# Recommendation kernel: one gather of 128 per step of the item stage as 128 single-row transfers from SyncE and ScalarE

## The chip, the cores and the metric

The kernel runs on one core of one Trainium2 chip. The metric is the device time of one execution in microseconds (us); smaller is better. The engines are TensorE (PE), VectorE (DVE), ScalarE (ACT), GpSimd (POOL) and SyncE (SP). Transfers between DRAM and the on-chip memory are carried by 16 DMA engines. SP, ACT and POOL can each issue transfers.

## The reference

The inputs are 16384 users with a history of 100 items each and one target item, a table of 32 neighbours for each of 50001 items, and tables of embeddings. First every item gets two attention results over its neighbours:

```
def _neighbor_attn(E, near_full):
    V = E[near_full]                                     # 50001 x 32 x 32
    scores = einsum('nd,nkd->nk', E, V) / sqrt(32)
    w = softmax(scores, axis=-1)
    return einsum('nk,nkd->nd', w, V)
a_sus = _neighbor_attn(E_in, near_full)
a_inf = _neighbor_attn(E_out, near_full)
h = concat([E_hist[history], a_sus[history], a_inf[history]])   # 16384 x 100 x 128
t = concat([E_tgt[target], a_inf[target], a_sus[target]])       # 16384 x 128
z = relu(einsum('bld,hd->blh', h * t[:, None, :], W1) + b1)
exp_A = exp(einsum('blh,h->bl', z, W2[0])) * ((history != target) & (history != 0))
attn = exp_A / sum(exp_A, -1) ** 0.5
s = sum(h * attn[..., None])                             # one number
pred = sigmoid(cosine(s everywhere, t))                  # 16384
```

## The kernel before, in words

The program has two stages, one after the other: the **item stage**, which writes a row of 129 numbers per item into a table in DRAM, and the **user stage**, which gathers those rows for every user's history. Only the item stage is changed.

The two embedding tables E_in and E_out lie side by side in one table `egeo` in DRAM, 64 numbers (256 bytes) per item. The 50001 items are cut into 391 tiles of 128 items. Sixteen tiles make a group (`it`), for which `load` fetches the neighbour indices `nidx` in one transfer. Four tiles of a group make a **step** (`s`); there are 99 steps, the first 96 of four tiles, the last three of four, two and one (steps 96, 97, 98). A step's buffer `v` holds, for each of its 128 x 4 items, the 32 neighbours' rows of `egeo`; there are three such buffers in turn.

`gather(s)` fills `v` with indirect transfers from POOL. One of them (here: one gather) fetches one neighbour `k` for the 128 items of one tile `i`: 128 rows of 256 bytes. A step of four tiles takes 128 gathers. Then VectorE's `product(s)` multiplies `v` by the items' own rows (`own`, which ACT first copies into `small`, L162), and `attended(s)` does the rest on VectorE: sums (L181), maximum, subtraction, an exponential on ACT (L199), weights times `v` (L201), the sum over neighbours (L218), the division and the row's total (L227). `written(s)` has ACT copy half of the row (L232) and SP write the finished rows (`ttab` at L233, `table` at L236).

The order on every engine is the order of the calls, which the loop below writes out by hand. Each engine's instructions run in that order, and a semaphore holds an instruction until what it needs is done. The first gather of step `s` waits for the product of step `s - 1` (a dependency added by hand, "the gathers pause here"). The gathers of POOL share eight completion counters (DMASW0 to 7) in turn, and the transfers of SP and ACT together share eight others (DMAHW0 to 7). A transfer waits until the one before it on its counter has landed.

In one turn of the loop the calls are: the product of `s - 1`, the gathers of `s`, the index load of the next group (once in four steps), the own rows of `s + 2` (`own_of`), then the rest of the attention of `s - 1` and its writing.

In the user stage POOL gathers 128 rows of 516 bytes at a time from `table` (L358), 20 for each fifth of a block of 128 users, and one gather of target rows per block (L328); VectorE, SP (L403, L409, L455), TensorE (L418) and ACT work on them.

Of the kernel before, what the change touches and what calls it, by code (L numbers as in the profile page):

```python
# [10 lines left out]
F32 = mybir.dt.float32  # L11
I32 = mybir.dt.int32
U8 = mybir.dt.uint8
E = mybir.EngineType
AF = mybir.ActivationFunctionType
ALU = mybir.AluOpType
AX = mybir.AxisListType

P = 128
ITEMS = 50001  # L20
K = 32
G = 32
# [9 lines left out]
NSUB = 16  # L32
NT = -(-ITEMS // P)
ROWS = NT * P
STEP = 4

UC = B // P
BSUB = 4
# [19 lines left out]
def kernel(  # L58
# [13 lines left out]
    nc = tc.nc  # L72
# [4 lines left out]
    table = nc.dram_tensor("table_0", [ROWS, W], F32, kind="Internal").ap()  # L77
# [10 lines left out]
    def rows_of(t, it):  # L88
        n = min(NSUB, NT - it * NSUB)
        r = it * NSUB * P  # L90
        return t[r : r + n * P, :].rearrange("(p j) d -> p j d", j=n)

    steps = []
    for s in range(0, NT, NSUB):
        n, j = min(NSUB, NT - s), 0
        while j < n:
            left = NT - s - j
            m = min(STEP, n - j) if left > STEP else (left + 1) // 2
            steps.append((s // NSUB, j, m))
# [3 lines left out]
    with (  # L103
# [7 lines left out]
        its = {}  # L111
        subs = {}
# [4 lines left out]
        def load(it):  # L117
            n = min(NSUB, NT - it * NSUB)
            nidx = n_in.tile([P, NSUB, K], I32, name="nidx")
            nc.sync.dma_start(nidx[:, 0:n, :], rows_of(near, it))  # L120
            its[it] = nidx

        def copied(it):
            r0 = it * P * NSUB
            r1 = min(r0 + P * NSUB, ITEMS - 1)
            nc.sync.dma_start(ttab[r0:r1, 0:DE], etgt[r0:r1, :])
            if r1 == ITEMS - 1:
                nc.sync.dma_start(ttab[r1:ITEMS, 0:DE], etgt[r1:ITEMS, :])

        def own_of(s):  # L130
            it, j, m = steps[s]
            own = n_s.tile([P, STEP, 2 * G], F32, name="own", bufs=3)
            nc.sync.dma_start(own[:, 0:m, :], rows_of(egeo, it)[:, j : j + m, :])
            row = n_s.tile([P, STEP, W + G], F32, name="row", bufs=4)
            nc.sync.dma_start(row[:, 0:m, 1 : 1 + DE], rows_of(ehist, it)[:, j : j + m, :])
            subs[s] = {"own": own, "row": row}

        def gather(s):
            it, j, m = steps[s]
            v = n_v.tile([P, STEP, K, 2 * G], F32, name="v")  # L140
            subs[s]["v"] = v
            landed = subs[s]["landed"] = [
                nc.gpsimd.indirect_dma_start(  # L143
                    out=v[:, i, k, :],
                    out_offset=None,
                    in_=egeo,
                    in_offset=bass.IndirectOffsetOnAxis(ap=its[it][:, j + i, k : k + 1], axis=0),
                )
                for i in range(m)
                for k in range(K)  # L150
            ]
            if s > 0:
                tc.add_manual_dep(
                    landed[0].ins, subs[s - 1]["made"].ins.name, SYNC, reason="the gathers pause here"
                )

        def product(s):
            it, j, m = steps[s]
            u = subs[s]
            v, own = u["v"], u["own"]  # L160
            near_own = small[:, s % 2, 0 : m * 2 * G].rearrange("p (i d) -> p i d", i=m)
            nc.scalar.copy(near_own, own[:, 0:m, :])  # L162
            prod = n_p.tile([P, STEP, K, 2 * G], F32, name="pw")
            made = nc.vector.tensor_tensor(  # L164
                prod[:, 0:m],
                v[:, 0:m],
                near_own.rearrange("p i (o d) -> p i o d", o=1).to_broadcast([P, m, K, 2 * G]),
                ALU.mult,
            )
            for gone in u["landed"][:-1]:  # L170
                covered(made, gone)
            u["made"], u["prod"] = made, prod

        def attended(s):
            it, j, m = steps[s]
            u = subs[s]
            v, own, row, prod = u["v"], u["own"], u["row"], u["prod"]
            ex = small[:, s % 2, STEP * 2 * G : STEP * 2 * G + m * K * 2]
            low = small[:, s % 2, STEP * (2 * G + 2 * K) : STEP * (2 * G + 2 * K) + 2 * m]
# [49 lines left out]
        def written(s):  # L229
            it, j, m = steps[s]  # L230
            row = subs.pop(s)["row"]
            nc.scalar.copy(row[:, 0:m, W : W + G], row[:, 0:m, 1 + DE : 1 + DE + G])  # L232
            nc.sync.dma_start(  # L233
                rows_of(ttab, it)[:, j : j + m, DE:D], row[:, 0:m, 1 + DE + G : W + G]
            )
            nc.sync.dma_start(rows_of(table, it)[:, j : j + m, :], row[:, 0:m, 0:W])  # L236

        def covered(one, other):
            tc.declare_no_dep(one.ins, other.ins, reason="a later wait or one engine's order covers it")

        load(0)
        own_of(0)
        own_of(1)
        gather(0)
        copied(0)
        ps_c = held.enter_context(tc.tile_pool(name="ps_c", bufs=1, space=bass.MemoryType.PSUM))
        small = ps_c.tile([P, 2, 1024], F32, name="small")
        for s in range(len(steps) + 1):
            if s > 0:
                product(s - 1)  # L250
            if 0 < s < len(steps):
                gather(s)
            if s < len(steps):
                it, j, m = steps[s]
                if j == STEP and it + 1 < NITER:
                    load(it + 1)
                    copied(it + 1)
            if s + 2 < len(steps):
                own_of(s + 2)
            if s > 0:  # L260
                attended(s - 1)
                written(s - 1)

    pool = tc.tile_pool(name="uconst", bufs=1)
    const = ctx.enter_context(pool)
# [25 lines left out]
    def ring(name, n, *shape):  # L291
        return [u_h.tile([P, *shape], F32, name=f"{name}{i}") for i in range(n)]

    rows = ring("h", HB, LQ, W)
# [11 lines left out]
    with (  # L306
# [184 lines left out]
        for s in range(last + LAG + NCH):  # L491
            c, k = divmod(s, NCH)
            if s < last:
                if k == 0 and c % BSUB == 2 and 0 < c // BSUB and c // BSUB + 1 < UC // BSUB:
                    history_of(c // BSUB + 1)
                if k == 1 and c + 1 < USERS:
                    target_rows(c + 1)
                gather(s)
                blocks(s)
                move(s)  # L500
                if k == 3 and c + 1 < USERS:
                    target_work(c + 1)
            done, left = divmod(s - LAG - NCH, NCH)
            if 0 <= done < USERS and left == 0:
                weights(done)
            if s < last:
                hidden(s)
            if 0 <= s - LAG < last:
                partial(s - LAG)
                if (s - LAG) % NCH == NCH - 1:  # L510
                    folded((s - LAG) // NCH)
            if 0 <= done < USERS and left == 1:
                u = ended(done)
                waiting = (done, u)
            if 0 <= done < USERS and left == 2:
                summed(*waiting)
# [79 lines left out]
```

## Time and profile before

| What | Value |
|---|---|
| time, median of 3 runs | 35657.56 us (35654.25 to 35670.82) |
| the profiled execution's own time | 35666.41 us |
| its span, first to last instruction | 35664.6 us |
| item stage, to the last of its gathers | about 17500 us |
| user stage and the end | about 18160 us |
| gathers of the item stage (L143) | 12512 |
| gathers of the user stage (L358, L328) | 12928 |

The profile is of one execution. Its page gives the busy time of each engine, and the costliest groups of instructions by line: busy time, mean of one in ns, then the time for which the engine stood idle just before them and what ended most of it. Other views give the busy time of each engine in a stretch of the span, or the instructions in the order of time: start, duration, engine, line, operation, what is written and read, and in brackets the idle time before. SPq marks a transfer issued by SP: its time there is that of issuing it. Registers, waits and issuing are not counted as busy.

### The profile page before, as it was taken

To read this page: it belongs to the slowest core of one execution; us is meant where nothing else is said; L and a number is where in the kernel's file an instruction comes from. 1 tells how busy PE (TensorE), PEld (TensorE's weight loads), DVE (VectorE), ACT (ScalarE), POOL (GpSimd) and SP (SyncE) were. 2 spreads that over 40 slices of the span, in tenths; PEclk is the share of its full clock that TensorE was granted. 3 is DMA by queue.
4 is the path that set the end of the run, shared out by engine and by line. 5 is a ranking of instruction groups with operands and counts; after the bars stand their busy time and mean duration, and the time that the engine had idled before them with its cause. 6 is when DMAs were issued, how large, how long until landed. Compare 5 with 4: busy or idle time off the path is not lost.

```text
span 35664.6 us, 55636 instructions
## 1 busy us (share of the span) xinstructions
PE 5285.3 (15%) x6659; PEld 1829.6 (5%) x6659; DVE 11590.6 (32%) x5232; ACT 3500.3 (10%) x2864; POOL 25112.7 (70%) x25446
## 2 busy tenths in 40 slices
PE   0000000000000000000022222232222322222222
PEld 0000000000000000000001111111111111101011
DVE  2222222222222222222344444434444444444444
ACT  0000000000000000000011111111111111111112
POOL 7777777777777777777777666676666666667666
PEclk9999999999999999999865556666566655656556
DMA  1111111111111111111244444444444444444444
GB/s 31 28 28 28 29 28 28 28 29 28 28 28 29 28 28 28 29 28 27 66 140 139 141 140 142 142 136 141 140 142 141 141 140 141 142 138 144 139 140 138
DMA packets 1528347, 3043.73 MB, mean 85 GB/s; under 512 B 641056, under 2 KB 708256, under 8 KB 1446048
## 3 DMA queue, kind: packets, MB, share of 16 engines
q1 hardware_dynamic: 713888, 1774.76, 16.7%
q0 software_dynamic: 814080, 1265.42, 14.1%
q14 instruction: 325, 2.66, 0.0%
q8 instruction: 54, 0.88, 0.0%
HBM read 2154.17 MB, written 890.36 MB: 85 GB/s over the span
## 4 chain that ended last, share of the span: by engine, by line
issue 40%; POOL 22%; another core or an unknown queue 21%; DVE 10%; ACT 4%; PE 1%; DMA 1%; SPq 0%; ACTq 0%; POOLq 0%; DVEq 0%
POOL v L143 13%; POOL h L358 9%; ACT z L426 3%; DVE pw L164 2%; DVE att L218 2%; DVE pw L201 1%; DVE sc L181 1%; DVE x L374 1%; PE zb L418 1%; DVE xb L388 1%; DVE zT L435 1%; DVE part L436 1%; ACT z L429 0%; PE za L418 0%
## 5 line engine op out<-in xcount | busy, mean ns | idle before, releaser
L358 POOL DMA_INDIRECT h<-table,hidx x12800 | 12305.2, 961 | 5632.1 <-issue 4769.4
L143 POOL DMA_INDIRECT v<-in_egeo_dram,nidx x12512 | 12686.1, 1014 | 4810.1 <-issue 3767.3
L164 DVE TENSOR_TENSOR pw<-v,small 128x8192 f32<-128x8192 f32 (+1 forms) x99 | 849.5, 8580 | 13307.6 <-DMA v<-in_egeo_dram,nidx 13307.6
L418 PE MATMUL za<-xT,w1T 128*128 128x512 f32 x3840 | 3165.9, 991 | 10408.6 <-issue 3777.7
L435 DVE STREAM_TRANSPOSE zT<-z 128x2560 f32<-128x2560 f32 x640 | 1812.4, 2832 | 5759.5 <-ACT z L429 4637.2
L488 PE MATMUL tp<-ident,w_sb 128*128 128x128 f32 x1 | 0.4, 448 | 17510.0 <-DMA hidx<-in_history_dram 17510.0
L374 DVE TENSOR_TENSOR x<-h,tp 128x2560 f32<-128x2560 f32 x640 | 1801.3, 2814 | 2394.6 <-DMA h<-table,hidx 1960.4
L418 PE MATMUL zb<-xT,w1T 128*128 128x512 f32 x2560 | 2002.0, 926 | 2434.7 <-issue 1784.8
L426 ACT ACTIVATE z<-za,b_sb 128x1536 f32<-128x1536 f32 x640 | 986.3, 1541 | 8673.7 <-remote 5545.8
L388 DVE STREAM_TRANSPOSE xb<-x 128x2560 f32<-128x2560 f32 x640 | 1820.9, 2845 | 0.0
L436 DVE TENSOR_REDUCE part<-zT 128x80 f32<-128x2560 f32 x640 | 1804.8, 2820 | 21.9
L418 PEld LDWEIGHTS za<-xT,w1T 128*128 128x128 f32 x3840 | 1145.6, 318 | 12453.9 <-issue 9065.4
L429 ACT ACTIVATE z<-z,w_sb 128x2560 f32<-128x2560 f32 x640 | 1554.0, 2428 | 20.9
L199 ACT ACTIVATE small<-sc 128x256 f32<-128x256 f32 (+1 forms) x99 | 38.1, 385 | 15116.3 <-DVE sc L193 8230.1
L218 DVE TENSOR_REDUCE att<-pw 128x256 f32<-128x8192 f32 (+1 forms) x99 | 1347.2, 13608 | 0.0
L426 ACT ACTIVATE z<-zb,b_sb 128x1024 f32<-128x1024 f32 x640 | 713.0, 1114 | 5741.8 <-remote 4112.7
L488 PEld LDWEIGHTS tp<-ident,w_sb 128*128 128x128 f32 x1 | 0.2, 183 | 17509.9 <-issue 17509.9
L201 DVE TENSOR_TENSOR pw<-v,small 128x8192 f32<-128x8192 f32 (+1 forms) x99 | 849.3, 8579 | 51.1 <-issue 37.0
L418 PEld LDWEIGHTS zb<-xT,w1T 128*128 128x128 f32 x2560 | 662.6, 282 | 3673.0 <-issue 2864.4
L181 DVE TENSOR_REDUCE sc<-pw 128x256 f32<-128x8192 f32 (+1 forms) x99 | 849.3, 8578 | 3.4
L467 DVE TENSOR_TENSOR ea<-ea,keep 128x100 f32<-128x100 f32 x128 | 33.9, 265 | 2488.2 <-issue 2099.2
L232 ACT COPY row<-row 128x128 f32<-128x128 f32 (+1 forms) x99 | 29.6, 299 | 2295.9 <-issue 1737.4
(53 smaller groups left out, 1124.5 us busy)
## 6 DMA issues: line engine op xcount, KB each, us to landing
there<-xb SPq DMA_DIRECT2D x2560, 320.0 KB
xT<-there SPq DMA_DIRECT2D x640, 1280.0 KB
h<-table,hidx POOLq DMA_INDIRECT x12800
v<-in_egeo_dram,nidx POOLq DMA_INDIRECT x12512
table<-row SPq DMA_DIRECT2D x97, 258.0 KB
own<-in_egeo_dram SPq DMA_DIRECT2D x97, 128.0 KB
row<-in_ehist_dram SPq DMA_DIRECT2D x97, 128.0 KB
ttab<-row SPq DMA_DIRECT2D x97, 128.0 KB
```

The lines of the kernel that those rows point to most:

```text
L143: nc.gpsimd.indirect_dma_start(out=v[:, i, k, :], out_offset=None, in_=egeo, in_offset=bass.IndirectOffsetOnAxis(ap=its[it][:, j + i, k : ...
L164: made = nc.vector.tensor_tensor(prod[:, 0:m], v[:, 0:m], near_own.rearrange("p i (o d) -> p i o d", o=1).to_broadcast([P, m, K, 2 * G]), ...
L181: nc.vector.tensor_reduce(sc[:, 0:m].rearrange("p i k t -> p (i k t)"), prod[:, 0:m].rearrange("p i k (t d) -> p (i k t) d", t=2), AX.X, A ...
L218: nc.vector.tensor_reduce(att[:, 0:m], wv[:, 0:m].rearrange("p i k d -> p i d k"), AX.X, ALU.add)
L358: landed[s, q] = nc.gpsimd.indirect_dma_start(out=rows[s % HB][:, q, :], out_offset=None, in_=table, in_offset=bass.IndirectOffsetOnAxis(a ...
L374: made = nc.vector.tensor_tensor(x, h[:, :, 1:W], u["tp"].to_broadcast([P, LQ, D]), ALU.mult,)
L388: turn = nc.vector.transpose(xb.rearrange("p b q j -> p q b j"), x.rearrange("p q (b i) -> p q b i", b=Q))
L418: one = nc.tensor.matmul(z_ps[:, m - lo, :], w1T, xT[:, m * COLS : (m + 1) * COLS], start=True, stop=True,)
L426: nc.scalar.activation(z[:, lo * COLS : hi * COLS], z_ps.rearrange("h m n -> h (m n)"), AF.Relu, bias=b1_sb)
L429: nc.scalar.activation(z, z, AF.Copy, scale=w2_sb)
L435: nc.vector.transpose(zT.rearrange("p x i -> p (x i)"), zr[s % ZB])
L436: nc.vector.tensor_reduce(parts[c][:, :, k * LQ : (k + 1) * LQ], zT.rearrange("p (a q) i -> p a q i", a=Q), AX.X, ALU.add,)
```

## The change

In the steps 1 to 98, of the gathers of the first tile the last one (neighbour 31) is left out. In its place each of the 128 rows is fetched by a transfer of its own, of 256 bytes, from an address that is held in a register: the rows 0 to 63 by SP, 64 to 127 by ACT. The column of indices is loaded a second time per group, transposed (`ridx`, one tile per partition), and VectorE multiplies it by 256 into byte addresses (`addr`). SP and ACT load 16 addresses at a time from `addr` into registers and then issue 16 transfers. They do so for the step after the one whose gathers run. SP issues the first 32 of its rows ahead of the attention and writing of the step before, and the other 32 behind them; ACT issues all 64 behind them.

```
+RUN = 16
+ROWB = 2 * G * 4
+EARLY = {E.SP: P // 4, E.Activation: 0}
+FETCH = (E.SP, E.Activation,)
...
             nc.sync.dma_start(nidx[:, 0:n, :], rows_of(near, it))
+            ridx = n_in.tile([NSUB, P], I32, name="ridx")
+                nc.sync.dma_start(ridx[0:n, :], rows_of(near, it)[:, :, K - 1].rearrange("p j -> j p"))
+            addr = n_in.tile([NSUB, P], I32, name="addr")
+            nc.vector.tensor_scalar(addr[0:n, :], ridx[0:n, :], float(ROWB), None, ALU.mult)
...
+        def by_row(s):
+            return 1 if s > 0 else 0
+
+        def space(s):
+            subs[s]["v"] = n_v.tile([P, STEP, K, 2 * G], F32, name="v")
+
+        def fetch_rows(s, e, q0, q1):
+            it, j, m = steps[s]
+            if not by_row(s):
+                return
+            for q in range(e * P // 2 + q0, e * P // 2 + q1, RUN):
+                _, found = nc.values_load_multi_w_load_instructions(
+                    its[it]["addr"][j : j + 1, q : q + RUN],
+                    engines=[FETCH[e]],
...
+                for i, value in enumerate(found):
+                    engine_of[FETCH[e]].dma_start(
+                        subs[s]["v"][q + i : q + i + 1, 0, K - 1, :].bitcast(U8),
+                        flat[ds(value, ROWB)].rearrange("(o b) -> o b", o=1),
+                    )
...
                 for i in range(m)
-                for k in range(K)
+                for k in range(K - (i < by_row(s)))
...
             if s + 2 < len(steps):
                 own_of(s + 2)
+            if s + 1 < len(steps):
+                space(s + 1)
+                for e in range(len(FETCH)):
+                    fetch_rows(s + 1, e, 0, EARLY[FETCH[e]])
             if s > 0:
                 attended(s - 1)
                 written(s - 1)
+            if s + 1 < len(steps):
+                for e in range(len(FETCH)):
+                    fetch_rows(s + 1, e, EARLY[FETCH[e]], P // 2)
```

Three places of the built program show what moves. The lines of the changed program have other numbers: L161 loads addresses, L169 is a single-row transfer, L180 a gather. First ACT, between the row copy of one step and the exponential of the next. Before:

```order
L162 COPY small<-own 128x256
L199 ACTIVATE small<-sc 128x256
L232 COPY row<-row 128x4x32
L162 COPY small<-own 128x256
L199 ACTIVATE small<-sc 128x256
```

Now:

```order
L269 COPY row<-row 128x4x32
L161 TENSOR_LOAD addr
L169 DMA v<-in_egeo_dram 1x256 x16
L161 TENSOR_LOAD addr
L169 DMA v<-in_egeo_dram 1x256 x16
L161 TENSOR_LOAD addr
L169 DMA v<-in_egeo_dram 1x256 x16
L161 TENSOR_LOAD addr
L169 DMA v<-in_egeo_dram 1x256 x16
L199 COPY small<-own 128x256
L236 ACTIVATE small<-sc 128x256
```

Four loads and 64 transfers now stand between the row copy and the copy of the own rows that the next product reads. Second SP, in one turn of the loop, from the own rows of a later step on. Before:

```order
L133 DMA own<-in_egeo_dram 128x256
L135 DMA row<-in_ehist_dram 128x4x64
L233 DMA ttab<-row 128x4x64
L236 DMA table<-row 128x4x129
L133 DMA own<-in_egeo_dram 128x256
```

Now:

```order
L142 DMA own<-in_egeo_dram 128x256
L144 DMA row<-in_ehist_dram 128x4x64
L161 TENSOR_LOAD addr
L169 DMA v<-in_egeo_dram 1x256 x16
L161 TENSOR_LOAD addr
L169 DMA v<-in_egeo_dram 1x256 x16
L270 DMA ttab<-row 128x4x64
L273 DMA table<-row 128x4x129
L161 TENSOR_LOAD addr
L169 DMA v<-in_egeo_dram 1x256 x16
L161 TENSOR_LOAD addr
L169 DMA v<-in_egeo_dram 1x256 x16
```

Half of SP's rows stand ahead of the two writes and half behind them, and the next step's own rows behind those. Third POOL, where one step ends and the next begins (with the counters that each gather waits for; DVE is the product). Before:

```order
L143 DMA v_90<-in_egeo_dram,nidx_80 128x64 [waits DMASW7_49]
L143 DMA v_231<-in_egeo_dram,nidx_80 128x64 [waits DMASW0_49,DVE_49]
L143 DMA v_231<-in_egeo_dram,nidx_80 128x64 [waits DMASW1_49]
L143 DMA v_231<-in_egeo_dram,nidx_80 128x64 [waits DMASW2_49]
L143 DMA v_231<-in_egeo_dram,nidx_80 128x64 [waits DMASW3_49]
```

Now, from the fourth step on:

```order
L180 DMA v_1310<-in_egeo_dram,nidx_80 128x64 [waits DMASW4_49]
L180 DMA v_1854<-in_egeo_dram,nidx_755 128x64 [waits DMAHW3_49,DMAHW4_49,DMAHW2_49,DMAHW5_49,DMAHW1_49,DMAHW6_49,DMAHW0_49,DMAHW7_49,DMASW5_49,DVE_49]
L180 DMA v_1854<-in_egeo_dram,nidx_755 128x64 [waits DMASW6_49]
L180 DMA v_1854<-in_egeo_dram,nidx_755 128x64 [waits DMASW7_49]
L180 DMA v_1854<-in_egeo_dram,nidx_755 128x64 [waits DMASW0_49]
```

A step's first gather now waits for the eight counters of SP's and ACT's transfers too: the single rows of the step that last used this buffer. The product of a step waits for the same eight counters, for its own rows.

More of the change, by code (lines that the diff above doesn't have):

```diff
@@ L120, in load @@
             nc.sync.dma_start(nidx[:, 0:n, :], rows_of(near, it))
-            its[it] = nidx
+            ridx = n_in.tile([NSUB, P], I32, name="ridx")
+            with nc.allow_non_contiguous_dma(reason="one index of each item, for single rows"):
+                nc.sync.dma_start(ridx[0:n, :], rows_of(near, it)[:, :, K - 1].rearrange("p j -> j p"))
+            addr = n_in.tile([NSUB, P], I32, name="addr")
+            nc.vector.tensor_scalar(addr[0:n, :], ridx[0:n, :], float(ROWB), None, ALU.mult)
+            its[it] = {"nidx": nidx, "addr": addr}
         def copied(it):
@@ L136, in own_of @@
             subs[s] = {"own": own, "row": row}
+        flat = egeo.rearrange("r d -> (r d)").bitcast(U8)
+        engine_of = {E.SP: nc.sync, E.Activation: nc.scalar}
+        def by_row(s):
[10 more added lines that the diff above has]
+                    engines=[FETCH[e]],
+                    min_val=0,
+                    max_val=(ITEMS - 1) * ROWB,
+                    skip_runtime_bounds_check_because="every index is a row of the table",
+                )
[3 more added lines that the diff above has]
+                        flat[ds(value, ROWB)].rearrange("(o b) -> o b", o=1),
+                    )
         def gather(s):
             it, j, m = steps[s]
-            v = n_v.tile([P, STEP, K, 2 * G], F32, name="v")
-            subs[s]["v"] = v
+            if "v" not in subs[s]:
+                space(s)
+            v = subs[s]["v"]
             landed = subs[s]["landed"] = [
@@ L146, in gather @@
                     in_=egeo,
-                    in_offset=bass.IndirectOffsetOnAxis(ap=its[it][:, j + i, k : k + 1], axis=0),
+                    in_offset=bass.IndirectOffsetOnAxis(ap=its[it]["nidx"][:, j + i, k : k + 1], axis=0),
                 )
                 for i in range(m)
-                for k in range(K)
+                for k in range(K - (i < by_row(s)))
             ]
```

## The prediction

> **What bounds the kernel now.** I read the page's share by engine first, then the groups by line, then busy time by stage, then the order of time across one step of the item stage.
>
> ```profile
> PE 5285.3 (15%) x6659; PEld 1829.6 (5%) x6659; DVE 11590.6 (32%) x5232; ACT 3500.3 (10%) x2864; POOL 25112.7 (70%) x25446
> ...
> L358 POOL DMA_INDIRECT h<-table,hidx x12800 | 12305.2, 961 | 5632.1 <-issue 4769.4
> L143 POOL DMA_INDIRECT v<-in_egeo_dram,nidx x12512 | 12686.1, 1014 | 4810.1 <-issue 3767.3
> L164 DVE TENSOR_TENSOR pw<-v,small 128x8192 f32<-128x8192 f32 (+1 forms) x99 | 849.5, 8580 | 13307.6 <-DMA v<-in_egeo_dram,nidx 13307.6
> ```
>
> POOL is the busiest engine, nearly all of its work is gathers, and in the item stage VectorE's product (L164) waits 13307.6 us for their data. The stages by time:
>
> ```profile
> 0.00:17500.00 17500.00, 0.00 (x0) 0.00 (x0) 4121.43 (x981) 95.68 (x296) 12686.83 (x12518) 1.00 0.13 28
> 17500.00:35664.00 18164.00, 5285.32 (x6659) 1829.64 (x6659) 7469.19 (x4252) 3404.59 (x2568) 12425.88 (x12928) 0.61 0.48 140
> ```
>
> The columns are the stretch, its length, then busy time of PE, PEld, DVE, ACT and POOL, the clock, the DMA share and GB/s. In the item stage ACT works 95.68 us of 17500, VectorE 4121, and the DMA engines are 13% busy. So the item stage lasts as long as POOL takes over its gathers. How long one takes is seen in a single step, in the order of time:
>
> ```profile
> 1050.08 1.09 POOL L143 DMA_INDIRECT v<-in_egeo_dram,nidx  x1 [0.30 <-issue]
> 1052.62 8.69 DVE L164 TENSOR_TENSOR pw<-v,small 128x8192 f32<-128x8192 f32 x1 [136.12 <-DMA v<-in_egeo_dram,nidx]
> ...
> 1061.58 0.95 POOL L143 DMA_INDIRECT v<-in_egeo_dram,nidx  x1 [10.40 <-DVE pw L164]
> 1062.83 0.94 POOL L143 DMA_INDIRECT v<-in_egeo_dram,nidx  x1 [0.30 <-issue]
> ...
> 1143.96 1.01 POOL L143 DMA_INDIRECT v<-in_egeo_dram,nidx  x1 [0.30 <-issue]
> 1145.28 1.09 POOL L143 DMA_INDIRECT v<-in_egeo_dram,nidx  x1 [0.30 <-issue]
> 1146.68 1.10 POOL L143 DMA_INDIRECT v<-in_egeo_dram,nidx  x1 [0.30 <-issue]
> ...
> 1240.79 0.95 POOL L143 DMA_INDIRECT v<-in_egeo_dram,nidx  x1 [10.42 <-DVE pw L164]
> ```
>
> A step lasts 1240.79 - 1061.58 = 179.21 us: a pause of 10.4 us behind the product, then 66 gathers at (1143.96 - 1061.58) / 66 = 1.248 us each, then the rest at 1146.68 - 1145.28 = 1.40 us. And 179.21 / 128 = 1.400: the step is as long as 128 gathers at the slow pace with no pause at all. What the pause takes is given back by the quick ones behind it. The program's start says how much can be saved up so:
>
> ```profile
> 174.02 0.94 POOL L143 DMA_INDIRECT v<-in_egeo_dram,nidx  x1 [10.47 <-DVE pw L164]
> ...
> 326.30 0.94 POOL L143 DMA_INDIRECT v<-in_egeo_dram,nidx  x1 [0.30 <-issue]
> 327.55 1.06 POOL L143 DMA_INDIRECT v<-in_egeo_dram,nidx  x1 [0.30 <-issue]
> 328.91 1.09 POOL L143 DMA_INDIRECT v<-in_egeo_dram,nidx  x1 [0.31 <-issue]
> ```
>
> There the 128 gathers of step 0 and 123 of step 1 go quickly, to 327.55. The first began at 3.9, so 251 gathers took 323.6 us where 251 x 1.40 is 351.4: a reserve of 27.8 us, some 20 gathers. The rule that I take from these rows is a long-run price of 1.400 us per gather, with pauses up to the reserve free of charge. The user stage, with other rows and nearly four times the DMA share, has the same price: (12305.2 + 5632.1) / 12800 = 1.401. All 25440 gathers at 1.400 make 35616 of the span's 35664.6 us.
>
> **The change, part by part.** *Removed:* one gather in each of the steps 1 to 98, so 98 x 1.400 = **137.2 us**. The lower price would be the quick one, 98 x 1.248 = 122.3 us, if the count of slow ones did not fall; nothing if the long-run price were not paid per gather (second rival). I take 1.400, since both stages keep it whatever the pauses are.
>
> *Added on ACT:* 64 single-row transfers and 4 loads of 16 addresses per step, between its last item of a step (the row copy, L232) and the small copy for the next product (L162):
>
> ```profile
> 1094.91 0.30 ACT L232 COPY row<-row 128x128 f32<-128x128 f32 x1 [23.48 <-issue]
> 1094.91 0.69 DVE L227 TENSOR_REDUCE row<-row 128x4 f32<-128x512 f32 x1
> 1095.11 0.37 ACT L162 COPY small<-own 128x256 f32<-128x256 f32 x1
> 1095.23 0.37 SPq L233 DMA_DIRECT2D ttab<-row  x1
> 1095.28 0.94 POOL L143 DMA_INDIRECT v<-in_egeo_dram,nidx  x1 [0.30 <-issue]
> 1095.69 0.46 SPq L236 DMA_DIRECT2D table<-row  x1
> ```
>
> ACT is done at 1095.2, which is 33.9 us after the product's end (1052.62 + 8.69 = 1061.31). Then the small copy (0.4 us) is wanted only for the next product, whose 8.7 us end the cycle. With r for one row, its share of the loads included, ACT's round is 33.9 + 64 r + 0.4 + 8.7 us, against 127 x 1.400 = 177.8 us on POOL. It fits up to r = (177.8 - 43.0) / 64 = **2.11 us**. No row of before shows a transfer from ACT, one of a single row, or a load of addresses. The nearest rows are SP's small ones:
>
> ```profile
> 1.18 0.42 SPq L133 DMA_DIRECT2D own<-in_egeo_dram  x1
> 1.65 0.43 SPq L135 DMA_DIRECT2D row<-in_ehist_dram  x1
> 2.12 0.51 SPq L133 DMA_DIRECT2D own<-in_egeo_dram  x1
> 2.67 0.43 SPq L135 DMA_DIRECT2D row<-in_ehist_dram  x1
> 3.15 0.61 SPq L126 DMA_DIRECT2D ttab<-in_etgt_dram  x1
> 3.80 2.81 SPq L133 DMA_DIRECT2D own<-in_egeo_dram  x1
> ...
> 17508.10 0.43 SPq L477 DMA_DIRECT2D b_sb<-in_b_dram  x1
> ...
> L133 SPq DMA_DIRECT2D own<-in_egeo_dram x99: 421/1303/2922, 1.2 to 17048.3; - x99
> ...
> 35651.10 2.41 SPq L455 DMA_DIRECT2D score<-flat  x4
> 35654.87 0.29 ACT L461 ACTIVATE ea<-score 128x100 f32<-128x100 f32 x1 [3.79 <-DMA score<-flat]
> ```
>
> One behind the other they start every 0.47 us (1.18 to 1.65, 2.12), and the 0.5 KB one (b_sb) costs 0.43 as well, so size hardly matters; the four of score take 0.60 each. The dear ones (2.81; median 1.303 and at most 2.922 for own) stand behind wide transfers: the 2.81 behind a 512 KB one. A 256-byte row is nearest to b_sb and score. There is also a wait: the transfers of SP and ACT share eight completion counters, so each engine has four in flight where both issue. The last score issued ends at 35653.51 and its reader starts 1.36 us later; with its own issue that is about 2 us from issue to data, over four some 0.5 us per row. I take r = 0.6 with 2 us, a guess, for each load: 64 x 0.6 + 8 = 46 us, and a round of 89 us. The cost on the path is nothing; the cover is the 134.8 us in which ACT has no other work. Both ends stay: 0.47 x 64 = 30 us, and 2.92 x 64 = 187 us, which breaks the cover.
>
> *Added on SP:* the same 64 and 4, half of them ahead of the write of the finished rows (ttab, table) and half behind. At r = 0.6 they take 46 us of a step of 178 in which SP otherwise issues four to six transfers. The first half needs no result of the step at hand and runs while SP would wait for ACT's row copy; the second half puts the own and row loads about 20 us later, and those are read two steps on. On POOL's pace the rows above show nothing: beside SP's two issues at 1095.23 and 1095.69 the gather at 1095.28 still takes 0.94.
>
> *Added on VectorE:* 25 multiplications of 16x128 numbers behind a product, under 0.7 us each (the 128x512 reduction above takes 0.69), and a wait for the loaded column of indices. Behind it stands the rest of the attention work, and behind that ACT's exponential and SP's writes. The product that POOL waits for has already gone ahead, so this eats only the cover.
>
> *Added waits:* the product now also waits for the rows, which were issued a step earlier, and a step's first gather for the same counters. POOL's own work is 127 x 1.248 = 158.5 us with the pause of 10.4, so the pause may grow by 177.8 - 168.9 = 8.9 us before it costs anything. Some ten satisfied waits do not make that; nor does the load of one more column per four steps.
>
> Sum: -137.2 us. The profiled execution took 35666.4 us around its span of 35664.6 and stands 8.9 us above the median of 35657.6; the sum is 35529.2 on its time, and **35520 us** on the median, 0.38% less.
>
> **The rivals.** *ACT becomes the bound (slower).* Above 2.11 us per row the round of ACT is the step; above (179.2 - 43.0) / 64 = 2.13 the change loses. At 2.5 us it is 203.0 us per step, 23.8 more than now over 96 full steps, so 37,940 us; at 2.92 about 40,500. For it speaks that own's issue did take up to 2.92 us, that ACT waits on counters that SP's transfers hold, and that a transfer with its address from a register is in no row. Against it speak b_sb and the run at 0.47. *No gain, because the rows take from the same store as the gathers did.* If 128 rows cost what one gather did, the time stays at 35658. [...] Against this rival stands that the DMA engines are 13% busy here and the price was 1.401 at 48%: POOL's issuing, not the moving, is what is short. *The saving at the quick pace:* 35535 us, on the same side as my forecast; for it speaks only that a step has both paces.
>
> **How the numbers follow.** No change is within 0.2%, about 71 us, as far as a measurement of this kernel can tell. The forecast of 137 us (its own range 35505 to 35545) has 0.76, the quick-pace saving 0.04, no gain 0.07, ACT as the bound 0.13. So faster 0.80, same 0.07, slower 0.13. Leaving out the slower rival, whose price is far away, the range runs from 35500 to 35662 and takes in no gain.
>
> **What would show it.** The gather of the item stage should count 12414, a step should last 177.8 us with some 66 quick gathers, and the product should go on waiting for a gather of POOL's queue. ACT should show 64 transfers per step, done some 50 us behind its row copy, and idle after. I am wrong if ACT's transfers stand 2 us apart or reach the next product, if POOL's pause exceeds 19 us, or if gathers beside the rows take longer than 1.40.

## The result and the profile after

| | before | changed | ratio (95% interval) |
|---|---|---|---|
| median | 35658.85 us | 36726.51 us (4 runs, 36725.94 to 36726.8) | 1.0299 (1.0281 to 1.0317) |

The changed kernel is 1068 us slower; 35520 us was forecast, 138 us faster. The prediction was wrong in size and in sign.

One thing has to be known to read the numbers below. The experiments ran on several chips, and these are of two kinds, told apart by the time of the kernel before: about 35,660 us on three occasions (the pair above is one) and about 33,760 us on four, with at most 0.13% between runs of a kind. Below they are called the *slow chips* and the *quick chips*. One quick chip came twice, and none was met as both; whether a chip can change its kind no run shows. Every ratio compares runs on one chip.

Groups of the page, changed kernel (columns as before):

```profile
PE 5315.3 (14%) x6659; PEld 1840.2 (5%) x6659; DVE 11593.2 (32%) x5257; ACT 3508.7 (10%) x2864; POOL 24201.3 (66%) x25348
...
q10 hardware_dynamic: 12544, 1.63, 0.0%
...
L180 POOL DMA_INDIRECT v<-in_egeo_dram,nidx x12414 | 11715.1, 944 | 6854.7 <-issue 3787.1
...
L201 DVE TENSOR_TENSOR pw<-v,small 128x8192 f32<-128x8192 f32 (+1 forms) x99 | 849.3, 8579 | 14375.0 <-ACT small L199 13682.1
...
L199 ACT COPY small<-own 128x256 f32<-128x256 f32 (+1 forms) x99 | 37.0, 373 | 14191.4 <-DMA v<-in_egeo_dram 14191.4
```

The 98 gathers are gone (12414), and those left are cheaper, 944 ns against 1014. POOL is busy 911 us less, but it sits idle 6855 us ahead of its gathers where it was 4810. The product no longer waits for gathers but for ACT's copy of the own rows, and that copy stands 14191 us behind "DMA v", ACT's own stretch of single-row transfers. q10, a queue that the page of before does not list, holds ACT's rows: 1.63 MB, of which 6272 rows of 256 bytes make 1.61. By stage:

```profile
0.00:18573.00 18573.00, 0.00 (x0) 0.00 (x0) 4121.57 (x1006) 105.44 (x296) 11715.82 (x12420) 1.00 0.12 27
18573.00:36725.00 18152.00, 5315.27 (x6659) 1840.23 (x6659) 7471.66 (x4252) 3403.29 (x2568) 12485.44 (x12928) 0.61 0.48 140
```

The item stage grew by 1073 us, and the user stage is as long as before. One step in the order of time, ACT, SP, VectorE's product and POOL's first gather:

```profile
9110.65 12.05 SPq L169 DMA_DIRECT2D v<-in_egeo_dram  x32
...
9150.49 0.30 ACT L269 COPY row<-row 128x128 f32<-128x128 f32 x1 [23.47 <-DVE att L255]
9152.41 145.50 ACTq L169 DMA_DIRECT2D v<-in_egeo_dram  x64
9155.75 87.49 SPq L169 DMA_DIRECT2D v<-in_egeo_dram  x32
9297.95 0.38 ACT L199 COPY small<-own 128x256 f32<-128x256 f32 x1 [147.16 <-DMA v<-in_egeo_dram]
9298.36 8.69 DVE L201 TENSOR_TENSOR pw<-v,small 128x8192 f32<-128x8192 f32 x1 [147.18 <-ACT small L199]
...
9307.32 0.94 POOL L180 DMA_INDIRECT v<-in_egeo_dram,nidx  x1 [31.96 <-DVE addr L129]
```

ACT's 64 rows take 145.50 us, 2.27 each. Only then can it do the 0.4 us copy, and the product follows at once: ACT's round is the step. POOL's last gather ended at 9307.32 - 31.96 = 9275.36, 23 us before the product starts, and its pause is 32 us instead of 10.4. SP's first 32 rows fall into such a pause and cost 0.38 each; its other 32 run beside gathers and cost 2.73. The instructions at that line:

```profile
L169 ACTq MOVE v<-in_egeo_dram x6272: 1/700/1399, 7.6 to 18527.5; - x196
L169 ACTq DMA_DIRECT2D v<-in_egeo_dram x6272: 1/699/1402, 7.6 to 18527.5; - x196
L169 SPq MOVE v<-in_egeo_dram x6272: 2/554/1424, 10.3 to 18515.3; - x196
L169 SPq DMA_DIRECT2D v<-in_egeo_dram x6272: 1/689/1400, 10.5 to 18515.3; - x196
```

(Duration in ns, least/median/most, then first and last start.) Each row is two instructions: a MOVE that puts the address in a register, and the transfer. While gathers run, successive ones on an engine start 1.40 us apart, so a row is 2.80 us. The rows alone make 1.61 of q10's 1.63 MB, so the MOVE carries next to no data, and still it is held like the transfer (medians 700 and 699 ns). Nor does SP's own issuing hold ACT: SP pauses from 9253 on, and ACT's next eight MOVEs, beside POOL's last gathers, still start 19.6 / 7 = 2.80 us apart.

```profile
9252.45 0.71 SPq L135 DMA_DIRECT2D ttab<-in_etgt_dram  x1
9298.35 0.35 SPq L142 DMA_DIRECT2D own<-in_egeo_dram  x1
```

```profile
L169 ACTq MOVE v<-in_egeo_dram x8: 690/700/709, 9253.2 to 9272.8; - x8
```

### The profile page after: what moved, and what is told of

Read it like the earlier page. It is cut to its first block, busy times and chain, and to the rows that moved or that the text cites. A ratio compares the mean times of both kernels' runs of the same rounds, so it can differ in the third digit from the quotient of the medians.

```text
span 36725.0 us, 82581 instructions
## 1 busy us (share of the span) xinstructions
PE 5315.3 (14%) x6659; PEld 1840.2 (5%) x6659; DVE 11593.2 (32%) x5257; ACT 3508.7 (10%) x2864; POOL 24201.3 (66%) x25348
## 3 DMA queue, kind: packets, MB, share of 16 engines
q10 hardware_dynamic: 12544, 1.63, 0.0%
## 5 line engine op out<-in xcount | busy, mean ns | idle before, releaser
L180 POOL DMA_INDIRECT v<-in_egeo_dram,nidx x12414 | 11715.1, 944 | 6854.7 <-issue 3787.1
```

The source lines that it names most:

```text
L180: nc.gpsimd.indirect_dma_start(out=v[:, i, k, :], out_offset=None, in_=egeo, in_offset=bass.IndirectOffsetOnAxis(ap=its[it]["nidx"][:, j + ...
```

## The experiments

**The slow chips: is the loss repeatable, and is it ACT's round?** The changed kernel again, e5_after:

> The changed kernel itself, measured again beside the kernel before. Theory D (the pace of the queues is a state of the chip on which a pair is measured: in the first measurement POOL, SP and ACT could start an instruction every 1.40 us in the long run, and in the runs e1 to e4 there was no such limit, gathers 1.248 us apart throughout and the kernel before at 33760 us): where the gathers of the kernel before run at 1.248 us throughout, the single rows take about 0.3 us and the changed kernel comes to 33760 - 98 x 1.248 = 33638 us; where they run at 1.40 us, to about 36726 us again. Theory A alone (single rows cost ACT 2.3 us wherever the change is measured, and only the four variants avoided that): about 1060 us slower than the kernel before on any chip.

Measured 36726.87 against 35660.38: 1.0299 (1.0281 to 1.0316). Once more beside the fixed-address form, e11_after:

> The changed kernel itself. Theory D: where the kernel before takes 33760 us (gathers 1.248 us apart throughout), 33760 - 98 x 1.248 = 33638 us, as its four variants there; where it takes 35660 us, 36727 us again. Theory A without the chip: about 1060 us slower than the kernel before in either case.

Measured 36725.13 against 35661.83: 1.0298 (1.0281 to 1.0315). The loss repeats to 2 us.

e12_fixed, each row's address written into the program in place of one loaded into a register:

```diff
-                _, found = nc.values_load_multi_w_load_instructions(
-                    its[it]["addr"][j : j + 1, q : q + RUN], ...
-                for i, value in enumerate(found):
+                for i in range(RUN):
+                    at = (q + i) * ROWB
...
-                        flat[ds(value, ROWB)].rearrange("(o b) -> o b", o=1),
+                        flat[at : at + ROWB].rearrange("(o b) -> o b", o=1),
```

> The kernel of e4 (fixed addresses, not the neighbours': no loads, no register moves; 64 transfers each on SP and ACT). Where the kernel before takes 35660 us: if the hold is one of instructions, a row falls from two instructions to one, from 2.80 to 1.40 us, ACT's round is 43 + 90 = 133 us, POOL is the bound at 177.8 us and the time is 35520 us; if it is one of transfers, a row keeps 2.80 us, only the loads go (4 x 1.4 us of a step of 190) and the time is about 36200 us. Where it takes 33760 us: 33638 us as in e4.

Measured **35550.51** against 35661.83 on the same chip as e11_after: 0.9968 (0.9955 to 0.998), 111 us faster. The rows are as many and as large; only the loads and the MOVEs are gone. Its instructions at the row's line, and ACT's order of time:

```profile
L163 ACTq DMA_DIRECT2D v<-in_egeo_dram x6272: 1/700/1397, 5.8 to 17355.8; - x196
```

```profile
9099.20 0.30 ACT L263 COPY row<-row 128x128 f32<-128x128 f32 x1 [23.48 <-issue]
9099.51 77.68 ACTq L163 DMA_DIRECT2D v<-in_egeo_dram  x62
9177.24 0.38 ACT L193 COPY small<-own 128x256 f32<-128x256 f32 x1 [77.74 <-issue]
9177.89 2.80 ACTq L163 DMA_DIRECT2D v<-in_egeo_dram  x2
```

```profile
L195 DVE TENSOR_TENSOR pw<-v,small 128x8192 f32<-128x8192 f32 (+1 forms) x99 | 849.4, 8580 | 13204.3 <-DMA v<-in_egeo_dram,nidx 13131.9
```

One instruction per row is still held (median 700 ns; 77.68 / 62 = 1.25 us per row; the two rows recorded behind the copy come up again under what stays open), but ACT's stretch falls from 145.5 to under 80 us, and the product waits for a gather of POOL's queue again (13131.9 of 13204.3). So the hold is one of instructions, not of bytes or rows, and ACT's round was the bound. SP's rows are held alike (32 of them in 44.80 us) and cost nothing.

e6_four, four gathers of every full step as rows (383 gathers less in all):

```diff
+MANY = 4
...
-            return 1 if s > 0 else 0
+            return 0 if s == 0 else MANY if steps[s][2] == STEP else 1
...
+            for t in range(by_row(s) if late else 1):
```

> Change against the changed kernel: four gathers per full step, one of each tile, instead of one, go to single rows, 256 each on SP and ACT (383 gathers in all instead of 98). Theory D where gathers run at 1.248 us: ACT's round is 43 + 256 x 0.31 + 16 loads at about 1.2 us = 142 us, below POOL's 124 x 1.248 + 10.5 = 165.3 us, so all 383 x 1.248 = 478 us are saved: 33282 us. Where queues run at 1.40 us per instruction: ACT's round is 43 + 256 x 2.3 to 2.8 us + 16 x 1.4, that is 650 to 780 us per step, and the time 80000 to 93000 us. Theory B (single rows cost the gathers something): less than 478 us saved.

Measured 44664.29 us, 1.2525 (1.2504 to 1.2546). Slower, as ACT's bound demands, but far below that expectation. The order of time, ACT and then POOL's first gather of a step:

```profile
9298.26 0.30 ACT L272 COPY row<-row 128x128 f32<-128x128 f32 x1 [23.48 <-DVE att L258]
9299.91 227.57 ACTq L172 DMA_DIRECT2D v<-in_egeo_dram  x256
9527.52 0.38 ACT L202 COPY small<-own 128x256 f32<-128x256 f32 x1 [228.97 <-DMA v<-in_egeo_dram]
```

```profile
9264.93 0.94 POOL L183 DMA_INDIRECT v<-in_egeo_dram,nidx  x1 [117.81 <-DVE pw L204]
```

256 rows in 227.57 us are 0.89 each, less than half the price in the changed kernel, because POOL now stands still for 117.81 us of the step. In that stretch, from some 19 us after the last gather on, about 24 rows per 10 us start on an engine (0.42 us each); while gathers run, 3.5 do. The hold is there beside gathers and for a while behind them, and not in the rest of the pause.

**The quick chips: edits of the changed kernel.** Four edits ran first, with the expectations below. They met a quick chip, where none of those numbers could come out as written.

e1_act_early, half of ACT's rows ahead of its row copy (`EARLY = {E.SP: P // 4, E.Activation: P // 4}` for `E.Activation: 0`):

> Change: 32 of ACT's 64 single rows are issued between its small copy and its exponential, where ACT has 18 us of its own idle time and POOL pauses for the product; nothing else moves. Theory A (ACT's round is the step: row copy, 64 rows at 2.27 us, small copy, product): the 32 early ones run at about 0.3 us each in POOL's pause, the other 32 at 2.8 us, so the round falls to about 33.9 + 90 + 9.1 = 133 us, POOL is the bound again at 127 x 1.400 = 177.8 us per step and the time is 35520 to 35560 us. Theory A with early rows that are not quick either (2.8 us each): they delay the exponential by some 70 us, the round is about 214 us and the time about 39000 us. Theory B (single-row transfers cost the gathers themselves, wherever they stand): the time stays near 36700 us.

e2_act_block, ACT's 64 rows as one transfer of fixed rows:

```diff
+            if FETCH[e] == E.Activation:
+                if q1 == P // 2:
+                    nc.scalar.dma_start(
+                        subs[s]["v"][e * P // 2 : (e + 1) * P // 2, 0, K - 1, :], egeo[0 : P // 2, :]
+                    )
+                return
```

> Change: ACT's 64 single rows of a step become one transfer of 64 consecutive rows (which are not the neighbours' rows: that part of the computation is left out); SP's 64 single rows stay. Theory A (ACT's round is the step): with ACT's round at about 45 us POOL is the bound again, 177.8 us per step, 35520 us; a little more if SP's 64 rows at up to 2.8 us (179 us) then become the step. Theory B (the transfers take from what the gathers need): half of the excess goes, so about 36100 us. Theory C (SP and ACT slow each other down): SP's rows come closer, 1.4 us instead of 2.8.

e3_sp_block, the same edit for SP (`E.SP`, `nc.sync`, ACT's rows left single):

> Change: SP's 64 single rows of a step become one transfer of 64 consecutive rows (not the neighbours' rows: left out); ACT's 64 single rows stay. Theory A (ACT's round is the step, and its pace does not come from SP): ACT's rows stay near 2.3 to 2.8 us and the time near 36700 us. Theory C (SP and ACT slow each other, by the shared counters or a shared issuing unit): ACT's rows fall to about 1.4 us, its round to 133 us, the time to 35520 us. Theory B: about 36100 us.

e4_fixed_address, the diff of e12_fixed:

> Change: the 128 single rows come from fixed addresses (not the neighbours' rows: left out), so no address is loaded and no register is set before a transfer; 64 transfers each on SP and ACT stay, with the same counters. If the slow pace is one of instructions (each instruction of the queue, the register move too, starts 1.40 us after the one before): 1.4 us per row, ACT's round 43 + 90 = 133 us, 177.8 us per step, 35520 us. If it is one of transfers (2.8 us each): only the loads go (4 x 1.4 = 5.6 us per step), so about 36170 us.

| on a quick chip | us | ratio |
|---|---|---|
| before | 33759.96 | |
| e1_act_early | 33639.7 | 0.9964 (0.995 to 0.9978) |
| e2_act_block | 33638.29 | 0.9964 |
| e3_sp_block | 33638.03 | 0.9964 |
| e4_fixed_address | 33638.74 | 0.9964 |

All gain 120 to 122 us, and 98 x 1.248 is 122.3. Four different edits with one time mean that none of them touches the bound there. They ran once more, meant for the other kind of chip:

> The kernel of e1 (32 of ACT's 64 rows between its small copy and its exponential, where POOL pauses). Where the kernel before takes 35660 us: in the changed kernel rows go at 0.3 us in the pause once the gathers have been still for some 16 us, and POOL's pause lasts 31 us there. If the pause stays long enough for that, 32 rows leave the slow stretch and the step falls to 177.8 us (35520 us). If with a shorter pause the rows stay slow, all 64 at 2.8 us make 179 us of every step with 4 loads and the copies, about 186 us per step, 36300 us. Where it takes 33760 us: 33638 us as in e1.

> The kernel of e2 (ACT's 64 single rows as one transfer of 64 consecutive rows, not the neighbours'; SP's 64 stay) on whatever chip it meets. Where the kernel before takes 35660 us (queues held to one instruction per 1.40 us while gathers run): theory A (ACT's round of 190 us is the step) says that POOL is the bound again, 127 x 1.400 = 177.8 us per step, 35520 to 35700 us. The rival, that SP's rows are as long a round (64 x 2.8 us + 4 loads + 4 transfers, about 190 us), says near 36700 us. Where the kernel before takes 33760 us: 33638 us as in e2.

> The kernel of e3 (SP's 64 single rows as one transfer of 64 consecutive rows, not the neighbours'; ACT's 64 stay). Where the kernel before takes 35660 us: theory A (ACT's rows are held by the gathers, not by SP) keeps 2.2 to 2.8 us per row on ACT and a time near 36700 us; theory C (SP and ACT hold each other) gives ACT's rows 1.4 us and 35520 us. Where it takes 33760 us: 33638 us as in e3.

> The kernel of e4 (fixed addresses, not the neighbours': no loads, no register moves; 64 transfers each on SP and ACT). Where the kernel before takes 35660 us: if the hold is one of instructions, a row falls from two instructions to one, from 2.80 to 1.40 us, ACT's round is 43 + 90 = 133 us, POOL is the bound at 177.8 us and the time is 35520 us; if it is one of transfers, a row keeps 2.80 us, only the loads go (4 x 1.4 us of a step of 190) and the time is about 36200 us. Where it takes 33760 us: 33638 us as in e4.

Another quick chip: 33638.96, 33636.43, 33637.69 and 33637.98 against 33759.1, all 0.9964 (0.995 to 0.9978, e7_early to 0.9979). On a slow chip the first three have no time; what e3_sp_block and e9_sp_block ask, whether SP's rows hold ACT's, is answered there by the trace of the changed kernel above. Whether the edits or the chip had removed the loss was told by the changed kernel itself, e14_after:

> The changed kernel itself, unaltered, for the case that it meets a chip on which the kernel before takes about 33760 us (gathers at 1.248 us each throughout); there it has not been timed yet. Theory A (the loss is made by ACT's rows at 2.80 us each, and these stand so only where every instruction of the ACT and SP queues is held 1.40 us beside the gathers): there the rows cost about 0.31 us each, as in the edited kernels, ACT's round ends under POOL's 127 gathers, and the time is 33638 us, 122 us under the kernel before (98 gathers of 1.248 us). Rival B (the edits of those kernels, the early fetch, the block, the fixed address, are what removed the loss): about 1065 us above the kernel before. On a chip where the kernel before takes 35660 us, both expect 36726 us.

Measured **33639.74** against 33760.45: 0.9964 (0.995 to 0.9978). Without any edit the loss is gone, so it goes with the chip. Order of time and instructions, to set beside those of the same program above:

```profile
9153.54 0.30 ACT L269 COPY row<-row 128x128 f32<-128x128 f32 x1 [23.48 <-DVE row L258]
9155.19 30.27 ACTq L169 DMA_DIRECT2D v<-in_egeo_dram  x64
9156.87 16.39 SPq L169 DMA_DIRECT2D v<-in_egeo_dram  x32
9185.49 0.38 ACT L199 COPY small<-own 128x256 f32<-128x256 f32 x1 [31.65 <-DMA v<-in_egeo_dram]
9188.33 11.70 SPq L169 DMA_DIRECT2D v<-in_egeo_dram  x32
...
9279.98 8.69 DVE L201 TENSOR_TENSOR pw<-v,small 128x8192 f32<-128x8192 f32 x1 [125.75 <-DMA v<-in_egeo_dram,nidx]
...
9288.94 0.94 POOL L180 DMA_INDIRECT v<-in_egeo_dram,nidx  x1 [10.49 <-DVE pw L201]
```

```profile
L169 ACTq MOVE v<-in_egeo_dram x6272: 29/29/37, 7.2 to 16442.8; - x196
L169 ACTq DMA_DIRECT2D v<-in_egeo_dram x6272: 213/213/508, 7.2 to 16442.9; - x196
```

The MOVE takes 29 ns and the transfer 213, with gathers running beside them. The 64 rows are issued in 30.27 us (0.47 each, loads included), ACT is ready 94 us before the product, and POOL's pause stays at 10.49.

e15_four, the edit of e6_four here:

> Four of each full step's gathers (383 in all) as single rows. On a chip where the kernel before takes 33760 us, theory A: ACT's round is 43 + 256 rows of 0.31 us + 16 loads of 1.2 us = 142 us, against POOL's 128 less 4 gathers of 1.248 us and its 10.5 us pause, 165 us: POOL stays the bound and the time falls by 383 x 1.248 = 478 us, to 33282 us. Rival (rows beyond the first 64 of a step collide with the gathers' transfers): above 33638 us. On a chip where the kernel before takes 35660 us, 44660 us as measured before.

Measured 33552.94: 0.9939 (0.9923 to 0.9956), 207 us under before where 478 was expected. The order of time on ACT, and VectorE's product:

```profile
9255.33 0.30 ACT L272 COPY row<-row 128x128 f32<-128x128 f32 x1 [23.48 <-DVE row L261]
9256.98 121.68 ACTq L172 DMA_DIRECT2D v<-in_egeo_dram  x256
9378.71 0.38 ACT L202 COPY small<-own 128x256 f32<-128x256 f32 x1 [123.07 <-DMA v<-in_egeo_dram]
...
9379.11 8.69 DVE L204 TENSOR_TENSOR pw<-v,small 128x8192 f32<-128x8192 f32 x1 [123.09 <-ACT small L202]
```

A row was not 0.31 us plus a load apart, but 121.68 / 256 = 0.475, as in e14_after. ACT's round, 33.6 + 1.7 + 121.7 + 0.4 + 8.7 = 166.1 us, lies just above POOL's 165.3 (124 x 1.248 + 10.5). A step takes 167.9 us on the mean (every fourth is some 4 us longer than the others) where e14_after takes 168.8. The product waits for ACT's copy again, so the same mechanism as on the slow chips ends the gain here, at four gathers' worth of rows per step in place of one. It is the fastest version measured on a quick chip; on a slow one it is the worst.

e16_act_block and e17_act_block were meant to tell on a slow chip whether ACT's rows alone bound:

> ACT's 64 rows of each step go as one transfer of 64 rows (of the first rows of the table, so that half of one column of each step is not what the reference gathers); SP's 64 stay single rows. On a chip where the kernel before takes 35660 us, theory A (ACT's round alone is the bound of the changed kernel): ACT's round is then 45 us, SP's 64 rows (32 of them in POOL's pause, 32 beside the gathers, 87 us) end under POOL's gathers, and the time is 35520 to 35560 us. Rival C (any hold on the row transfers of SP bounds as well): 36000 us or more. On a chip where the kernel before takes 33760 us: 33638 us, as measured before.

> ACT's 64 rows of each step go as one transfer of 64 rows (of the first rows of the table, so that half of one column of each step is not what the reference gathers); SP's 64 stay single rows. Meant for a chip where the kernel before takes 35660 us. Theory A (there ACT's round alone is the bound of the changed kernel): ACT's round is then about 45 us, SP's 64 rows (32 of them in POOL's pause, 32 beside the gathers, 87 us) end under POOL's gathers, and the time is 35520 to 35560 us. Rival C (a hold on the row transfers of SP bounds as well): 36000 us or more. On a chip where the kernel before takes 33760 us: 33638 us, as measured before.

Both met quick chips: 33636.34 against 33760.45 and 33634.15 against 33756.62, 0.9963 and 0.9964 (0.9949 to 0.9978). On a slow chip this form has no time.

e13_alternate and e18_alternate, rows in every second step, spread over two:

```diff
-            return 1 if s > 0 else 0
+            return s % 2
...
+            if 0 < s < len(steps) - 2 and by_row(s + 2):
+                space(s + 2)
+                for e in range(len(FETCH)):
+                    fetch_rows(s + 2, e, 0, P // 4)
```

> Every second step alone fetches one gather as rows (49 gathers less in place of 98), and of such a step's 128 rows half are issued one step earlier, so that ACT and SP issue 32 rows each beside the gathers of every step. Theory A: where a row costs ACT 2.80 us, its round is 43 + 32 x 2.80 + 2 x 1.40 = 135 us, under the 178 us of 127 gathers of 1.40 us: the rows are hidden, and the time falls by 49 x 1.40 = 69 us, to 35592 us, against 35660 us before. Rival C (it is the mere presence of row transfers beside the gathers that costs): half of the loss stays, about 36190 us. On a chip where the kernel before takes 33760 us: 49 x 1.248 = 61 us less, 33698 us.

> Every second step alone fetches one gather as rows (49 less in place of 98), half of them issued one step earlier, so that ACT and SP issue 32 rows each beside the gathers of every step. Meant for a chip where the kernel before takes 35660 us. Theory A: a row costs ACT 2.80 us there, its round is 43 + 32 x 2.80 + 2 x 1.40 = 135 us, under the 178 us of 127 gathers of 1.40 us: the rows are hidden, and the time falls by 49 x 1.40 = 69 us, to 35592 us. Rival C (it is the mere presence of row transfers beside the gathers that costs): half of the loss stays, about 36190 us. On a chip where the kernel before takes 33760 us: 33702 us, as measured before.

Quick chips as well: 33702.12 against 33760.45 and 33697.96 against 33756.62, 0.9983 (0.9973 to 0.9992). 49 gathers less give 58 us, half of what 98 give. Whether it beats the kernel before on a slow chip, which was its purpose, stays open.

## Why the prediction was wrong

*What failed is the term r, ACT's price of a row.* The prediction took 0.6 us and 2 us for each load, 46 us for ACT's stretch. The trace shows 145.5, and 147.1 with the gap behind the row copy: r = 2.30, above the 2.13 from which the change was said to lose. The four loads, guessed at 2 us each, were not it: ACT's take 0.70 us in the median. Two errors are in r. The price came from SP's rows at the start of the program, at the end of a stage and from b_sb, where no item gathers stand in the way. The group of own, quoted in the same fence, has 1.303 as its median; it was put down to wide transfers. The kernel before shows otherwise in the order of time, directly behind the ttab and table rows (1095.23, 1095.69) that the prediction quotes:

```profile
1098.74 1.40 SPq L133 DMA_DIRECT2D own<-in_egeo_dram  x1
1101.55 0.00 SPq L135 DMA_DIRECT2D row<-in_ehist_dram  x1
```

Beside gathers SP's third transfer starts 3 us after the second and the fourth 2.8 us after that. On a quick chip (e3_sp_block) SP's third and fourth behind the same two writes, also beside gathers, start 0.75 and 0.40 us apart:

```profile
9490.13 0.37 SPq L276 DMA_DIRECT2D ttab<-row  x1
9490.60 0.45 SPq L279 DMA_DIRECT2D table<-row  x1
9491.35 0.35 SPq L124 DMA_DIRECT2D nidx<-in_near_dram  x1
9491.75 0.45 SPq L127 DMA_DIRECT2D ridx<-in_near_dram  x1
```

So SP's queue was already held before the change: the first instructions of a stretch are quick, and the prediction priced r from such rows. For own's longest issue, 2.922, width may still be the reason, since the quick chip of e14_after has one of 2.829. Second, a row with its address in a register was counted as one instruction and is two. With one instruction, e12_fixed shows, even the hold would have left ACT's round under POOL's. On the quick chips, where no row is held, r is 0.47 with the loads, where the prediction's 46 us make 0.72. That chips differ so was not among the rivals: that the forecast comes near there, in sign and size, is luck.

*The formula for ACT's round held.* With r = 2.30 it gives 43.0 + 147.1 = 190.1 us, and the traced step is 9307.32 - 9117.17 = 190.15. The rival that ACT becomes the bound, at 0.13, is what happened on the slow chips, and its price follows: over the steps 2 to 96 the mean goes from 179.24 to 189.90, so 95 x 10.66 = 1013 us; the first step with rows is 37 us longer, and the second-last, which has half the gathers, 24 us (109.4 against 85.8, from the end of one product to the next); with -13 in the user stage and -1 in the last step the sum is 1060 us, the difference of the two spans.

*POOL's price of 1.400 us per gather held where it was read.* In e12_fixed the step is 177.94 us (127 x 1.400 = 177.8), 1.30 less than before, over 95 steps 123 us. The half step takes 25 of them back: its product waits for ACT's copy, so it lasts ACT's round, 111.0 us where the kernel before took 85.8, which the count of 98 equal savings left out. The user stage, which was not changed, adds 14, about as much as runs of the kernel before differ (35654 to 35671): 111.5 in all, against 137.2. On the quick chips the price in the item stage is 1.248 throughout, and the rival "quick pace" has the size, 122.3 us for 121 measured. So the price goes with the chip: 1.400 in before and in e12_fixed, 1.248 in e14_after.

*No gain from a shared store* fell. Issuing was what counted: on the slow chips ACT's stretch of it is 147.1 of a step's 190.15 us, and on the quick chips the rows gained 121 of the 122.3 us that 98 gathers are worth there.

*POOL beside the rows:* the forecast that SP's and ACT's issues do not delay gathers held (944 ns in after and in e14_after). VectorE's added work and the first gather's added waits cost nothing that can be seen: the pause on a quick chip is 10.49 us, where the kernel before has 10.40.

*Of the three signs named in advance*, two came on the slow chips: transfers more than 2 us apart that reach the next product, and a pause above 19 us. The third, slower gathers, did not.

What stays open is where the hold comes from. The traces show its shape: on the slow chips a queue instruction of ACT or SP starts 1.40 us after the last while gathers run, the two engines in turn on a grid of 0.70 us, the first few quick (in the step above ACT's first three rows start between 9152.4 and 9153.3), and quick again, 0.31 us a row, some 18 us after the last gather (the median of the changed kernel's steps); in the kernel before POOL's own gathers reach the same 1.40 after a reserve of about 20. What makes it was not shown. Nor do the records settle what is held: in e12_fixed's fence two of a step's 64 rows are recorded at 9177.89, behind the copy at 9177.24, though ACT's order has all 64 ahead of that copy. So a record can be later than the issue, and the traces alone do not tell which of the two is held; ACT does wait for it, as the changed kernel's step of 190.15 us shows.

## What to carry to other kernels

Price an instruction on an idle engine's queue from rows in which the neighbours' load is running, and take a group's median seriously before its best rows; count what a line issues in the trace's instructions, not in the program's calls. Before work is put on an idle engine, write its round and its break-even price beside the highest price that any row shows: with 2.13 against a seen 2.92, the number of instructions was the thing to cut. And when a gain hangs on issue prices, time it on more than one chip: the same program lost 3.0% on one kind and won 0.4% on the other.

## What the chip showed that was not expected

- The same program before takes 35,660 us on some chips and 33,760 on others, 5.3% apart. On the quick ones the item stage's gathers stay at 1.248 us (the 12414 of e14_after are busy for 944 ns on the mean, with 0.30 us between them), an ACT transfer of the same kernel has a median of 213 ns instead of 699, and TensorE is busy for less in the same work:

```profile
PE 4433.6 (13%) x6659; PEld 1730.5 (5%) x6659; DVE 11565.3 (34%) x5257; ACT 3496.6 (10%) x2864; POOL 23916.2 (71%) x25348
```

  PE's 4433.6 us (e14_after) stand against 5315.3 in the same kernel on a slow chip.
- A row with a register address: 0.24 us of instructions (29 + 213 ns, ACT in e14_after), 0.37 issued by SP alone (11.70 / 32, the same run), 0.47 to 0.51 where ACT and SP issue together (30.27 / 64 and 16.39 / 32), 2.80 beside gathers on a slow chip (the changed kernel).
- Work can make its neighbours cheaper by waiting: on the slow chip the longer pause brings POOL's remaining gathers back to 1.248 us each (944 ns mean busy), though it gains nothing by it.
